# A two-level Winograd projection: two more of q, k and v's seven products split into quarters

## The chip, the cores and the metric

One core of a Trainium2 chip runs the whole kernel. The metric is the time on the device, in microseconds (us); lower is better. Five engines work in parallel, each in the order of its own instruction list: TensorE (PE, matmuls into PSUM, with its weight loads shown as PEld), VectorE (DVE), ScalarE (ACT), GpSimd (POOL) and SyncE (SP, which issues the DMAs). They wait for each other through semaphores.

## The reference

64 batches of 256 nodes with 512 features pass two layers. Layer 0 multiplies by an adjacency matrix and a weight; layer 1 is masked attention with 8 heads of 64 features. Each layer has a layer norm and a ReLU in front and a residual around it.

```python
h = jnp.maximum(_layernorm(x, axis=-1), 0.0)
x = x + (jnp.einsum('bnd,do->bno', jnp.einsum('nm,bmd->bnd', adj, h), weight) + bias)
h = jnp.maximum(_layernorm(x, axis=-1), 0.0)
q = (h @ Wq + bq).reshape(b, n, H, HD)      # k and v likewise
scores = jnp.einsum('bqhd,bkhd->bhqk', q, k) / jnp.sqrt(jnp.float32(HD))
scores = scores + (1.0 - adj)[None, None, :, :] * -1000000000.0
attn = jax.nn.softmax(scores, axis=-1)
x = x + (jnp.einsum('bhqk,bkhd->bqhd', attn, v).reshape(b, n, d) @ Wo + bo)
```

All is float32.

## The kernel before

Batches go in groups of two (`GB`), so there are 32 groups (`NG`). Layer 0 runs over all groups first and leaves two results in DRAM per group: the residual and the transposed hidden activations. Layer 1 then runs over the groups. In iteration g it does, in this order: `attend(g, 0)`, loads by DMA, `score(g, 1)`, `queries_keys(g + 1)` (first q, then k), `attend(g, 1)`, `score(g + 1, 0)`, `values(g + 1)`, and `post(g)`, the output product. On TensorE a group is thus six stretches: q, k, attention, v, output product, attention.

Every 512 by 512 product of a weight with two batches is done by the Winograd form of Strassen's method: the weight and the activations are cut in halves (blocks a11 to a22 and b11 to b22), sums s1 to s4 and t1 to t4 of blocks are made once, and seven products of half size take the place of eight. A half-size product is four matmuls of 128 rows by 256 columns (`product`). From group 2 (`FIRST2`) on, `project2` does three of the seven (a12 b21, a22 t4 and s4 b22) by the same method once more: each becomes seven matmuls of 128 columns, on quarter blocks (`W2` for the weight, `Blocks` for the activations). `block_sums` makes the sums of the weight's quarters, once for each weight, in the tiles of `spare`; POOL makes those of the activations for each group (`block_hidden`, `block_outputs`).

Matmuls write to PSUM, which has eight banks; `bank` takes the one that has been free longest, `give` returns it. A result leaves a bank through ACT (`first`, which adds the bias of q and k) or through DVE (`add`, onto what is there already). `bank(..., seed=...)` lets ACT copy values into a bank, onto which matmuls then accumulate.

The order is written by hand. A `yield` in a projection ends a step; `run` calls `tick` after each, and `after(delay, fn)` puts work of other engines into the instruction list that many ticks later. What is placed like this around the projections:

- `score`: 16 matmuls into eight banks, DVE scales and masks each (`scalar_tensor_tensor`, L980), POOL subtracts `top` in four pieces (L986), ACT takes the exponentials (`exponent`, at the ticks of `exps`, 3, 4, 5 and 8), POOL adds pairs of keys (`key_sum`, L998).
- `attend`: the sums of the exponentials (pden) and the weighted values (po, two banks), TensorE. ACT copies pden to `den`, DVE inverts it in four pieces (`invert`, L1027), two of them at once and the others in `divide`, one tick later, which also makes the two quotients oT (L1045) and gives back po's banks. ACT's `note` reads the inverses for a check of range.
- The loads of h1T (hidden) and x1 (residual) rotate through four buffers of `xpool`.

Of the kernel before, what the change touches and what calls it, by code (L numbers as in the profile page):

```python
# [198 lines left out]
def kernel(  # L199
# [35 lines left out]
    dram = main.enter_context(tc.tile_pool(name="between", bufs=1, space=bass.MemoryType.DRAM))  # L235
    xpool = main.enter_context(tc.tile_pool(name="x", bufs=4))
    act = main.enter_context(tc.tile_pool(name="act", bufs=1))
# [10 lines left out]
    def bank(shape, name, seed=None):  # L248

        i = next(i for i in free_banks if seed is None or whole[i])  # L250
        free_banks.remove(i)
        t = psum.tile(shape, F32, tag=f"bank{i}", name=name)
        bank_of[id(t)] = (i, t)
        if seed is not None:
            nc.scalar.copy(t, seed[:, None, :].to_broadcast(shape))
        return t
# [34 lines left out]
    def load(g):  # L291
        X[g] = xpool.tile([P, T, D], F32, tag="x", name=f"x_{g}")
        for k in range(GB):
            for i in range(NI):
                nc.sync.dma_start(blocks_of(X[g], i, k), by_block(x[g * GB + k], i))
# [74 lines left out]

    L1 = {}

    def load_layer1(n):
        w, bias = {"q": (wq, bq), "k": (wk, bk), "v": (wv, bv), "o": (wo, bo)}[n]
        if n in "qk":
            L1[n] = load_weight(nc, const, w, f"w{n}_sb"), load_column(nc, const, bias, f"b{n}_c")
        elif n == "v":
            L1[n] = load_weight(nc, const, w, "wv_sb"), None
        else:


            bv_c = const.tile([P, DC], F32, name="bv_c")
            wo_sb = const.tile([P, DC, D], F32, name="wo_sb")
            wo_v = w.rearrange("(q h f r) o -> h r q f o", q=HQ, h=4, f=2)
            bv_v = bv.rearrange("(q h f r) -> h r q f", q=HQ, h=4, f=2)
            for h in range(4):
                for q in range(HQ):
                    nc.sync.dma_start(wo_sb[32 * h:32 * h + 32, 2 * q:2 * q + 2, :], wo_v[h, :, q])
                    nc.sync.dma_start(bv_c[32 * h:32 * h + 32, 2 * q:2 * q + 2], bv_v[h, :, q])
            L1[n] = wo_sb, load_row(nc.sync, const, bias, "bo_r"), bv_c  # L390
# [119 lines left out]

    def block_sums(n):

        todo = []
        for a in ONCE:
            w = W[n][a]
            def part(i, j):
                return w[:, j, i * P:(i + 1) * P]
            s1, s2, s4 = (spare.pop(0) for _ in range(3))
            W2[n, a] = dict(a11=part(0, 0), a12=part(0, 1), a22=part(1, 1), s1=s1, s2=s2, s3=part(1, 0), s4=s4)
            for o, p, q, op in ((s1, part(1, 0), part(1, 1), ALU.add), (s2, s1, part(0, 0), ALU.subtract),  # L520
                                (part(1, 0), part(0, 0), part(1, 0), ALU.subtract), (s4, part(0, 1), s2, ALU.subtract)):
                todo.append((nc.gpsimd.tensor_tensor, o, p, q, op))
        return todo

# [15 lines left out]

    def project2(n, halves, blocks, by_token, name, place, first, done=None, seeds=(), add_up=False):

        s = W[n]

        def part(t, i, k):

            m, h = (k, i) if by_token else (i, k)
            t = t if m is None else t[:, m:m + 1, :]  # L550
            return t.rearrange("p m (h j) -> p (m h) j", j=P) if h is None else t[:, :, h * P:(h + 1) * P]

        class Inner:
# [103 lines left out]
        for p, c in zip(inner, ((0, 0), (1, 0), (0, 1))):  # L657
            p.u3()
            p.add(p.sum, None, 1)
            give(p.shared, False)  # L660
            complete(*c)
        yield

# [189 lines left out]

    H1T, HH, HO = {}, {}, {}

    def load_hidden(g):
        H1T[g] = xpool.tile([P, GB, DC, N], F32, tag="x", name=f"h1T_{g}")
        for k in range(GB):
            nc.sync.dma_start(H1T[g][:, k].rearrange("p d n -> p (d n)").rearrange("p (i n) -> p i n", n=N // NI),
                              HT[g][:, :, :, k, :].rearrange("p d i n -> p (d i) n"))  # L860

    def load_residual(g):
        X[g] = xpool.tile([P, T, D], F32, tag="x", name=f"x1_{g}")
        nc.sync.dma_start(X[g], X1[g].rearrange("k (t p) d -> p (k t) d", p=P))
# [7 lines left out]
    H2, O2 = {}, {}  # L872

    def block_hidden(g, step):

        t = act.tile([P, GB, 4, P], F32, tag="t2", name=f"t2_{g}")
        t4 = act.tile([P, 4, P], F32, tag="t24", name=f"t24_{g}")
        x = H1T[g][:, :, 2:4, :].rearrange("p k c (n j) -> p k c n j", j=P)
        H2[g] = block_sums_of(x, t, HH[g], t4, nc.gpsimd, step)

# [10 lines left out]
    def block_sums_of(x, t, halves, t4, eng, step):  # L891
# [4 lines left out]
        return {"b21": Blocks(x[:, 0], t[:, 0]), "b22": Blocks(x[:, 1], t[:, 1]), "t4": last}  # L896

    def queries_keys(g):

        for n, store in (("q", Q), ("k", K)):  # L900
            store[g] = {}
            bias = L1[n][1]

            def first(o, ps, i, m=None):
                for c in range(2) if m is None else (m,):
                    to, src = (o[:, c, :], ps[:, c, :]) if m is None else (o, ps)
                    nc.scalar.activation(to, src, AF.Identity, bias=bias[:, 2 * i + c:2 * i + c + 1])

# [4 lines left out]

            if g < FIRST2:
                yield from project(W[n], HH[g], False, f"{n}_{g}", place, first)
            else:
                yield from project2(n, HH[g], H2[g], False, f"{n}_{g}", place, first)

    def values(g):
        v = act.tile([P, HQ, GB, NT, HF], F32, tag="yT0", name=f"v_{g}")  # L920
        V[g] = {(i, k): v[:, i, k] for i in range(HQ) for k in range(GB)}

        def first(o, ps, i, m=None):
            nc.scalar.copy(o, ps)

        def place(i, k):
            return V[g][i, k]

        if g < FIRST2:
            yield from project(W["v"], HH.pop(g), True, f"v_{g}", place, first)  # L930
        else:
            yield from project2("v", HH.pop(g), H2.pop(g), True, f"v_{g}", place, first)

# [30 lines left out]
    def score(g, qd, sum_delay, exps=(3, 4, 5, 8)):  # L964
# [3 lines left out]
        for c in range(2):  # L968
            for b in range(GB):
# [13 lines left out]
                if (g == NG - 1 or (g, qd) == (0, 0)) and c + b == 2:  # L983
                    after(2, lambda a: nc.vector.tensor_tensor(a, a, top_b, op=ALU.subtract), a)  # L984
                else:
# [14 lines left out]
    def attend(g, qd):  # L1000
# [25 lines left out]
        def invert(c):  # L1026
            nc.vector.reciprocal(rden[:, c * P:(c + 1) * P], den[:, c * P:(c + 1) * P])  # L1027

        early = 2 if g >= FIRST2 and (g, qd) != (NG - 1, 1) else 4
        for c in range(early):  # L1030
            invert(c)
        if qd == 0:

            last = g == NG - 1
            OT[g] = (xpool if last else act).tile([P, DC, GN], F32, tag="x" if last else "r", name=f"oT_{g}")
            HO[g] = Halves(f"o_{g}", [OT[g][:, :, k * N:(k + 1) * N] for k in range(GB)], 0 if last else 1)
# [4 lines left out]
        def divide():  # L1041
            for c in range(early, 4):
                invert(c)
            for f in range(2):
                nc.vector.tensor_tensor(OT[g][:, 2 * qd + f, :], po[f], rden, op=ALU.mult)  # L1045
                give(po[f])
            after(2 if (g, qd) == (NG - 1, 1) else 3, note)
            wait = 0
# [4 lines left out]
            elif g == NG - 2:  # L1053
                wait = 8
                after(7, HO[g].sums, nc.gpsimd, ("t3",))
                after(8, HO[g].sums, nc.vector, ("t2",))
                after(8, HO[g].sums, nc.gpsimd, ("t4",))
            else:
                HO[g].sums(nc.vector, ("t3", "t2"))
                HO[g].sums(nc.gpsimd, ("t4",))  # L1060
            if qd and g >= FIRST2:
                block_outputs(g, nc.gpsimd, wait + 1 if g >= NG - 2 else 2)

        after(1, divide)

# [70 lines left out]
    for g in range(NG):  # L1136
        attend(g, 0)
        load_residual(g)
        if g + 2 < NG:
            load_hidden(g + 2)  # L1140
        score(g, 1, *((5,) if g < NG - 1 else (3, (3, 4, 5, 6))))
        tick()
        if g == 0:
            for n, tag in ((4 * DC, "w0_sb"), (4, "w0_s1"), (4, "w0_s2"), (4, "w0_s4"), (4, "adjT"), (4, "b0_r")):
                t = const.tile([P, n, P], F32, tag=tag, name=f"spare_{tag}")
                spare.extend(t[:, i, :] for i in range(n))
        for n, at in (("q", 7),) if g == 0 else (("k", 1), ("v", 5)) if g == 1 else (("o", 2),) if g == 2 else ():
            for i, work in enumerate(block_sums(n)):
                after(at + i // 3, *work)
        if g + 1 < NG:  # L1150
            run(queries_keys(g + 1))
        else:
            last = post(g - 1, seed_outputs(g - 1))
            run(last, 6)
        attend(g, 1)
        if g + 1 < NG:
            score(g + 1, 0, 5)
            tick()
# [57 lines left out]
```

## Time and profile before

| | |
|---|---|
| median of three runs | 2659.16 us (2658.59 to 2660.33) |
| profiled execution | 2660.45 us, its span 2658.7 us |
| granted TensorE clock, mean | 0.999 |
| DMA | 211.04 MB, mean 79 GB/s |
| one group of layer 1 (g=14, 1488.47 to 1551.47) | 63.00 us: busy PE 63.00, DVE 43.71, ACT 21.29, POOL 47.03 |
| POOL's longest idle time in it, ahead of `score(14, 0)` | 15.11 us, until DVE's masked scores |

The span goes from the first to the last instruction of one profiled execution. Times inside it are counted from its start. A matmul's line in a timeline gives the start and the time until its result is there; matmuls overlap, so that the distance of two starts is the pace. Each float32 matmul shows as two passes, so x2 is one matmul of the code. A note such as "[0.58 <-POOL as L998]" gives the idle time ahead of an instruction and what ended it.

### The profile page before, as it was taken

What the parts mean: (1) busy time and instruction counts of PE and PEld (TensorE: products, weight loads), DVE (VectorE), ACT (ScalarE), POOL (GpSimd) and SP (SyncE); (2) the same over time, 40 slices, a digit from 0 to 9 for tenths busy, and PEclk for the clock granted to TensorE, in tenths of its full rate; (3) what the DMA queues carried; (4) which work ended last, traced back from release to release, by engine and by line L of the source; (5) the groups of instructions that cost most, each with busy time, mean ns of one, the idle gap of its engine ahead of it and who ended that gap; (6) DMA issues with size and microseconds to landing.
All of it is one profiled execution on the core that took longest, in us unless ns stands there. A gap on an engine that the chain in (4) does not pass through costs nothing. (4 is left out here: it accounts for less than half of the span.)

```text
span 2658.7 us, 51781 instructions
## 1 busy us (share of the span) xinstructions
PE 2624.0 (99%) x20076; PEld 2282.2 (86%) x20076; DVE 1869.5 (70%) x3864; ACT 970.5 (37%) x1875; POOL 1981.1 (75%) x1838
## 2 busy tenths in 40 slices
PE   7999999999999999999999999999999999999997
PEld 6999899998888888888888888888888888888886
DVE  5878888885467676667677676667677676666677
ACT  3445454443333333333333333333333333333332
POOL 5888888775788777777777777777777777777775
PEclk9999999999999999999999999999999999999999
DMA  5777666665122111111111111111222111111110
GB/s 132 199 193 187 172 166 175 175 158 127 34 60 51 49 49 48 49 49 49 49 48 49 49 49 49 49 48 51 62 66 62 50 49 48 49 49 49 49 48 34
DMA packets 281066, 211.04 MB, mean 79 GB/s; under 512 B 145904, under 2 KB 212976, under 8 KB 280816
## 3 DMA queue, kind: packets, MB, share of 16 engines
q1 hardware_dynamic: 280352, 207.15, 29.9%
q8 instruction: 161, 2.64, 0.4%
q14 instruction: 89, 0.73, 0.1%
q10 hardware_dynamic: 464, 0.52, 0.1%
HBM read 106.96 MB, written 100.66 MB: 78 GB/s over the span
## 5 line engine op out<-in xcount | busy, mean ns | idle before, releaser
L986 POOL TENSOR_TENSOR a<-a,top 128x1024 f32<-128x1024 f32 x253 | 591.2, 2369 | 478.0 <-DVE a L980 478.0
L980 DVE SCALAR_TENSOR_TENSOR a<-sc,maskT 128x512 f32<-128x512 f32 x512 | 311.8, 680 | 122.8 <-PE sc L974 122.8
L998 POOL TENSOR_TENSOR as<-a 128x512 f32<-128x512 f32 x256 | 318.5, 1276 | 3.0 <-ACT a L991 3.0
L991 ACT ACTIVATE a<-a 128x1024 f32<-128x1024 f32 x256 | 270.9, 1058 | 4.3 <-DVE a L984 2.3
L1027 DVE RECIPROCAL rest<-rest 128x128 f32<-128x128 f32 x256 | 224.3, 919 | 36.1 <-ACT rest L1023 36.1
L974 PE MATMUL sc<-q,k 64*128 64x256 f32 x2048 | 239.0, 383 | 0.0
L1014 PE MATMUL pav<-a,v 128*32 128x256 f32 x4096 | 233.6, 379 | 0.0
L974 PEld LDWEIGHTS sc<-q,k 64*128 64x128 f32 x2048 | 194.7, 187 | 44.9 <-issue 26.3
L1014 PEld LDWEIGHTS pav<-a,v 128*32 128x32 f32 x4096 | 133.4, 110 | 87.9
L1023 ACT ACTIVATE rest<-pden 128x512 f32<-128x512 f32 x64 | 38.2, 597 | 417.7 <-PE pden L1007 417.7
L665 DVE TENSOR_TENSOR k<-k,k 128x128 f32<-128x128 f32 (+1 forms) x300 | 96.0, 352 | 126.3 <-PE k L564 123.9
L42 DVE BATCH_NORM_STATS2 st<-x 128x6 f32<-128x512 f32 x256 | 173.1, 676 | 9.4 <-DMA x<-in_x_dram 7.2
L693 ACT ACTIVATE h<-x,nb,rs 128x512 f32<-128x512 f32 x128 | 93.9, 803 | 69.3 <-POOL nb L54 69.2
L820 ACT ACTIVATE h<-x,nb,rs 128x512 f32<-128x512 f32 x128 | 97.2, 808 | 52.2 <-POOL nb L54 49.0
L665 DVE TENSOR_TENSOR x<-o,x 128x128 f32<-128x128 f32 (+1 forms) x360 | 110.9, 349 | 3.4 <-PE o_24b L564 0.3
L665 DVE TENSOR_TENSOR q<-q,q 128x128 f32<-128x128 f32 (+1 forms) x300 | 96.0, 352 | 14.0 <-PE q L564 11.7
L665 DVE TENSOR_TENSOR v<-v,v 128x128 f32<-128x128 f32 (+1 forms) x300 | 95.3, 351 | 14.4 <-PE v L564 11.3
L754 POOL TENSOR_TENSOR hs<-h 128x512 f32<-128x512 f32 x31 | 39.4, 1270 | 73.8 <-ACT h L693 63.7
L446 POOL TENSOR_TENSOR t_o<-oT,t_o 128x512 f32<-128x512 f32 x62 | 79.2, 1277 | 12.3 <-DVE t_o L446 10.0
L446 POOL TENSOR_TENSOR t_y<-yT 128x512 f32<-128x512 f32 (+1 forms) x65 | 81.8, 1258 | 5.9 <-ACT yT L804 5.9
L446 POOL TENSOR_TENSOR t_h<-h1T,t_h 128x512 f32<-128x512 f32 x64 | 82.0, 1282 | 5.0
L52 POOL TENSOR_TENSOR rs<-rs,mhalf 128x2 f32<-128x2 f32 (+1 forms) x97 | 79.5, 820 | 8.1
(4808 smaller groups left out, 6981.8 us busy)
## 6 DMA issues: line engine op xcount, KB each, us to landing
x<-in_x_dram SPq DMA_DIRECT2D x256, 128.0 KB, 3.1
residual<-x SPq DMA_DIRECT2D x256, 128.0 KB, 2.5
hidden<-r SPq DMA_DIRECT2D x128, 256.0 KB, 4.4
h1T<-hidden SPq DMA_DIRECT2D x64, 512.0 KB, 9.7
x<-residual SPq DMA_DIRECT2D x32, 1024.0 KB, 7.7
out_dram<-x SPq DMA_DIRECT2D x62, 512.0 KB, 4.3
w_sb<-in_L_gnn_weight_dram SPq DMA_DIRECT2D x1, 1024.0 KB, 9.8
wq_sb<-in_L_gnn_Wq_dram SPq DMA_DIRECT2D x1, 1024.0 KB, 8.2
```

Of the source, the lines that this page charges most:

```text
L42: nc.vector.bn_stats(st, src)
L446: eng.tensor_tensor(self.t[n][:, c, :], self.operand(p, c), self.operand(q, c), op=ALU.subtract)
L665: nc.vector.tensor_tensor(o, ps, u, op=ALU.add)
L693: nc.scalar.activation(H0[g][:, t, :], xt[:, t, :], AF.Relu, bias=nb[:, t % n:t % n + 1], scale=rs[:, t % n:t % n + 1])
L820: nc.scalar.activation(h1[:, k * NT + t, :], xt[:, k * NT + t, :], AF.Relu, bias=nb[:, t:t + 1], scale=rs[:, t:t + 1])
L974: nc.tensor.matmul(ps[j][:, kt * N:(kt + 1) * N], k[j * HD:(j + 1) * HD, c, kt * P:(kt + 1) * P], q[j * HD:(j + 1) * HD, c, :], start=(kt ...
L980: nc.vector.scalar_tensor_tensor(a[:, j * NT:(j + 1) * NT, :].rearrange("p k n -> p (k n)"), ps[j], SCALE, maskT_f, op0=ALU.mult, op1=ALU.add)
L986: nc.gpsimd.tensor_tensor(a, a, top_b, op=ALU.subtract)
L991: nc.scalar.activation(a, a, AF.Exp)
L998: nc.gpsimd.tensor_tensor(AS[c, b], a4[:, :, 0, :], a4[:, :, 1, :], op=ALU.add)
L1014: nc.tensor.matmul(po[f][h * 32:(h + 1) * 32, b * N:(b + 1) * N], v[:, k, h * HD + f * 32:h * HD + f * 32 + 32], A[h // 2, b][:, (h % 2) * ...
L1027: nc.vector.reciprocal(rden[:, c * P:(c + 1) * P], den[:, c * P:(c + 1) * P])
```

## The change

`project2` stays for the output product. For q, k and v of groups 2 to 31 a new `project3` does five of the seven half-size products on quarters: the three of before, and a11 b11 and s3 t3 (called A1 and A7). That leaves two half-size products, s2 t2 and s1 t1. The order of steps is new: A1, A7 and A3 (s4 b22) have their first quarter in one shared bank `sa`, their other parts in o1, o7 and o3; A2 and A4 share `s24` and o2, pc. The sum of A1 is put together in the output tile c00 and then copied back by ACT as the seed of bank pa, on which s2 t2 and s1 t1 accumulate; c11 likewise seeds pc. Since A1 and A7 are now taken separately, q's and k's second bias is a difference (`DIFF`).

```diff
+    def project3(n, halves, blocks, by_token, name, place, first):
+        s, part = W[n], part_of(by_token)
+
+        def mm(o, p, a, b, start=False):
+            lhs, rhs = W2[n, p][a], blocks[BUILT[p]].operand(b)
+            if by_token:
+                lhs, rhs = rhs, lhs
+            nc.tensor.matmul(o[:, 0, :], lhs, rhs, start=start, stop=True, skip_group_check=True)
+
+        def own(o, p, start=True):
+            mm(part(o, 0, 0), p, "a12", "b21", start)
+            mm(part(o, 0, 1), p, "s4", "b22")
+            mm(part(o, 1, 0), p, "a22", "t4")
+
+        def more(o, src, i, k):
+            o = part(o, i, k)
+            add(o, src if src.shape[1] == o.shape[1] else src.to_broadcast([P, o.shape[1], P]), o)
+
+        def take(o, src, i, k, h):
+            first(part(o, i, k), src, h, i)
+
+        def own_added(o, t):
+            more(o, part(t, None, 0), None, 0)
+            more(o, part(t, 1, 1), 1, 0)
+
+        def own_taken(o, t, h):
+            first(part(o, None, 1), part(t, None, 1), h, None)
+            give(t)
+
+        c00, c01, c10, c11 = (place(i, k) for i in range(2) for k in range(2))
+        sa = bank([P, 4, P], f"{name}s")
+        a1, a7, a3 = (sa[:, i:i + 1, :] for i in range(3))
+        mm(a1, "a11", "a11", "b11", True)
+        mm(a7, "s3", "a11", "b11")
+        o1 = bank([P, 2, N], f"{name}o1")
+        own(o1, "a11")
+        o7 = bank([P, 2, N], f"{name}o7")
+        own(o7, "s3")
+        take(c00, a1, 0, 0, 0)
+        take(c11, a7, 0, 0, 1)
+        yield
+        mm(a3, "s4", "a11", "b11")
+        mm(a1, "a11", "s2", "t2")
+        mm(a7, "s3", "s2", "t2")
+        mm(part(o1, 1, 1), "a11", "s3", "t3")
+        mm(part(o7, 1, 1), "s3", "s3", "t3")
+        o3 = bank([P, 2, N], f"{name}o3")
+        own(o3, "s4")
+        take(c00, a1, 1, 0, 0)
+        take(c11, a7, 1, 0, 1)
+        take(c01, a3, 0, 0, None)
+        for o, t, h in ((c00, o1, 0), (c11, o7, 1)):
+            own_added(o, t)
+            own_taken(o, t, h)
+        yield
+        mm(a1, "a11", "s1", "t1")
+        mm(a7, "s3", "s1", "t1")
+        mm(a3, "s4", "s2", "t2")
+        mm(part(o3, 1, 1), "s4", "s3", "t3")
+        more(c00, a1, None, 1)
+        take(c01, a3, 1, 0, None)
+        pa = bank([P, 2, N], f"{name}a", seed=c00)
+        more(c11, a7, None, 1)
+        yield
+        o2 = bank([P, 2, N], f"{name}o2")
+        own(o2, "a12")
+        s24 = bank([P, 4, P], f"{name}s24")
+        a2, a4, c4 = (s24[:, i:i + 1, :] for i in range(3))
+        mm(a4, "a22", "a11", "b11", True)
+        mm(a2, "a12", "a11", "b11")
+        mm(a3, "s4", "s1", "t1")
+        take(c10, a4, 0, 0, None)
+        pc = bank([P, 2, N], f"{name}c", seed=c11)
+        more(c00, a2, 0, 0)
+        yield
+        product(pa, s, "s2", halves, "t2", by_token, start=False, stop=False)
+        first(part(c10, 1, 0), part(pa, 1, 0), None, 1)
+        first(part(c10, None, 1), part(pa, None, 1), None, None)
+        more(c10, part(pa, 0, 0), 0, 0)
+        own_added(c01, o3)
+        yield
+        own(pc, "a22", False)
+        mm(a2, "a12", "s2", "t2")
+        mm(part(o2, 1, 1), "a12", "s3", "t3")
+        mm(a4, "a22", "s2", "t2")
+        mm(c4, "a22", "s3", "t3")
...
+        own_taken(c01, o3, None)
+        more(c01, a3, None, 1)
+        give(sa, False)
+        yield
+        product(pa, s, "s1", halves, "t1", by_token, start=False)
...
```

The last two steps end with eleven more additions by DVE. Around the projection other work moves: the exponentials to later ticks, the quotient from one tick after `attend` to five (its two later inverses at ticks 1 and 4; A2's first addition stands between the last inverse and the quotient), the sums t11 and t33 for the new products on POOL, k's weight sums to DVE, and the order of the last group. h1T and x1 rotate through three buffers; the fourth keeps weight quarters.

```diff
-        score(g, 1, *((5,) if g < NG - 1 else (3, (3, 4, 5, 6))))
+        score(g, 1, *((7, (5, 6, 6, 7)) if second(g + 1) else (5,) if g < NG - 1 else (3, (3, 4, 5, 6))))
         tick()
+        if g + 2 < NG:
+            block_first(g + 2, 12)
...
+        delay = 5 if second(g + 1) else 4 if (g, qd) == (NG - 1, 0) else 1
...
-        after(1, divide)
+        if (g, qd) == (NG - 1, 1):
+            divide()
+        else:
+            if delay == 5:
+                after(1, invert, 2)
+                after(4, invert, 3)
+            after(delay, divide)
...
     def block_hidden(g, step):
 
+        H2[g]["t3"] = Blocks(HH[g].t["t3"].rearrange("p c (n j) -> p c n j", j=P),
+                             tmp.tile([P, 4, P], F32, tag="u", name=f"t33_{g}"))
+        after(step - 2, H2[g]["t3"].sums, nc.gpsimd)
...
-                wait = 8
-                after(7, HO[g].sums, nc.gpsimd, ("t3",))
-                after(8, HO[g].sums, nc.vector, ("t2",))
-                after(8, HO[g].sums, nc.gpsimd, ("t4",))
+                wait = 8 - delay
+                after(wait, HO[g].sums, nc.gpsimd, ("t3",))
+                after(wait, HO[g].sums, nc.vector, ("t2",))
+                after(wait, HO[g].sums, nc.gpsimd, ("t4",))
...
-            run(last, 6)
+            run(last, 5)
```

## The prediction

> **What bounds the kernel now.** I read the page's busy times first, then who waited for whom on TensorE, then the stretches of one group of two batches (g=14) by engine, then the timelines of its stages and of the last 60 us. The page:
>
> ```profile
> PE 2624.0 (99%) x20076; PEld 2282.2 (86%) x20076; DVE 1869.5 (70%) x3864; ACT 970.5 (37%) x1875; POOL 1981.1 (75%) x1838
> ```
>
> A busy share of 99% does not prove that TensorE is the limit, but the waits do: between 900 and 2600 us the list of TensorE's waits is empty. The stretches of one group are q, k, attention, v, output product, attention. Columns: time, then busy us (instructions) of PE, PEld, DVE, ACT, POOL.
>
> ```profile
> 1488.47:1500.17 11.70, 11.70 (x76) 10.87 (x75) 9.38 (x20) 7.25 (x16) 11.70 (x7) 1.00 0.60 119
> 1500.17:1511.86 11.69, 11.69 (x76) 10.75 (x74) 5.59 (x16) 4.61 (x11) 3.70 (x4) 1.00 0.00 0
> 1519.97:1531.67 11.70, 11.70 (x76) 10.88 (x75) 9.46 (x20) 7.29 (x15) 11.62 (x7) 1.00 0.00 1
> ```
>
> TensorE fills each; DVE is 80% busy in q and v, 48% in k. A group takes 63.0 us, so a shorter projection shortens the run by its own gain, as long as nobody makes TensorE wait. Its pace, from k's timeline (start, length; x8 is four matmuls in two passes each, x2 is one):
>
> ```profile
> 1500.17 1.89 PE L453 MATMUL k_14a<-h1T,wk_sb 128*128 128x256 f32 x8
> 1501.90 1.89 PE L453 MATMUL k_14c<-t_h,wk_sb 128*128 128x256 f32 x8
> ...
> 1505.36 0.38 PE L564 MATMUL k<-h1T,wk_sb 128*128 128x128 f32 x2
> 1505.58 0.39 PE L564 MATMUL k<-t_h,wk_sb 128*128 128x128 f32 x2
> ```
>
> Starts are 1.73 us apart for a product of four 256-column matmuls (0.4325 each) and 0.2225 us for one of 128 columns; a result is there 0.17 us after the next start. The four lines that decide how far the gain gets, around q's start at 1488.47 (DVE, DVE, POOL, ACT):
>
> ```profile
> 1486.06 4.87 DVE L980 SCALAR_TENSOR_TENSOR a<-sc,maskT 128x512 f32<-128x512 f32 x8 [2.01 <-PE sc L974]
> 1490.85 1.75 DVE L1027 RECIPROCAL rest<-rest 128x128 f32<-128x128 f32 x2
> 1488.40 9.32 POOL L986 TENSOR_TENSOR a<-a,top 128x1024 f32<-128x1024 f32 x4
> 1499.97 1.05 ACT L991 ACTIVATE a<-a 128x1024 f32<-128x1024 f32 x1
> ```
>
> DVE is busy with the scores until 2.4 us into q; POOL's four subtractions end 9.2 us into q, and the last exponential that needs them starts at 11.5. At the end of the run TensorE does wait:
>
> ```profile
> 2614.67 1.89 PE L453 MATMUL o_30c<-wo_sb,t_o 128*128 128x256 f32 x8
> 2620.59 3.56 PE L453 MATMUL o_30a<-wo_s,t_o 128*128 128x256 f32 x8 [4.03 <-DVE x L665]
> ...
> 2632.13 0.41 PE L1007 MATMUL pden<-as,ones 128*32 128x256 f32 x2 [0.58 <-POOL as L998]
> ```
>
> **The Trainium skill.** TensorE: Matmul & The Clock Gate, section "Wait — 56ns, not 53.3ns?", gives a fixed cost of about 2.5 ns per matmul beside its columns: halving columns nearly halves time. The trace agrees: 111 ns per 128-column pass, 216 per 256. The same page, "Why this matters for your kernels", warns of TensorE gaps above about 3 us, after which the clock is halved: agrees, the eight passes after the 4.03 us gap took 3.56 us where 1.89 is usual. PSUM — Partial Sum Buffer, "PSUM bank collisions raise a hardware error", says that two engines must not touch one bank at once, reads included, and that dependencies are added for it; so ACT and DVE take turns on a bank. In the trace DVE's add from k_14a waits for ACT's copy out of the same bank at 1511.70.
>
> **The gain.** project2 has four 256-column products (16 matmuls) and 21 small ones: 16 x 0.4325 + 21 x 0.2225 = 11.59 us, and 0.10 at the change of shape before q and v or behind k: the measured 11.70 and 11.69. project3 has 8 and 35: 3.46 + 7.79 = 11.25. Gain 0.345 per projection, 1.035 per group, over 30 groups (2 to 31) 31.1 us.
>
> **What it costs other engines**, per projection. DVE: 21 additions for 15. Spacings in the trace are 0.20, 0.33 and 0.60 us for 128, 256 and 512 columns (0.47 for 384): before 6, 6 and 2 and one of 384, 4.9 us; now 8, 9 and 4, 7.0. ACT: q and k 16 operations for 10, v 14 for 7, among them two seeds of 0.52: 1.2 to 1.4 us more. POOL: six more quarter sums per group, two sets of 1.76 us (the row of such a set runs 1486.64 to 1488.40). Per group DVE goes from 43.7 to about 50, POOL 47.0 to 50.5, ACT 21.3 to 25, of some 62.5. No engine becomes the bound by its sum. The order does matter.
>
> **The hand-over in q.** Times from q's first matmul; an engine starts 0.04 us after the one it waits for (the trace has 0.03 to 0.11). Step 1 (8 small matmuls) ends at 1.88, step 2 at 3.66, step 3 at 4.55. DVE is free of the scores and of one reciprocal at 3.25. It adds o1's two quarters, the second dependent on the first (0.42, 0.28): 3.98. ACT takes o1's other half in two biased pieces: 4.64. DVE adds A1's half: 5.09. ACT may then read the same bank for A3: 5.39. DVE adds A7's half, again from that bank: 5.85. Only then may TensorE write A3's third product there, at 5.90. It arrives at 5.66 (step 3, then 5 matmuls). Stall 0.24. The seed of pa (ACT, 5.29 to 5.87) is in time; later waits have 0.4 us or more.
>
> **In k** DVE is late from q's last additions (free at 14.3); the chain starts with ACT at the same time, and the same counting gives 0.14. ACT first has to be free: POOL's subtractions now start 1.76 later for the t3 set, plus what v saves, at 1.83, the fourth ends at 11.15; last exponential to 12.1, the note to 12.7, two pieces of A1 and A7 to 13.36. TensorE wants that bank at 13.37: 0.03. **In v** ACT's pieces are single copies: 0.11. Left per group 1.035 - 0.24 - 0.17 - 0.11 = 0.52, over 30 groups 15.5 us.
>
> Bounds: with no stall 1.035; with hops of 0.08 instead of 0.04, at some seven hops each (0.33, 0.26 and 0.21 of stall), and POOL 0.5 later, the stalls reach 1.3 and the group loses 0.3. I take 0.52, as most waits in the trace end within 0.04 us.
>
> **Moved work.** The quotient (two of 0.65, behind a reciprocal) goes from 4.2 us into v to 6.8 to 8.1. It holds two PSUM banks four steps longer: project3 needs sa, o1, o7, o3 before o1 is given back, and six are free. POOL's sums of oT start, as before, when its subtractions end at 8.3: nothing, by 0.2 us. If that cover went, POOL has 1.4 us until pden wants its key sums. h1T and the residual have three buffers for four: h1T(g+2) now follows post(g-1)'s output DMA (4.3 us) on SP's queue, and is wanted some 40 us later by POOL: nothing. t11 lies in POOL's 15 us gap before the scores: nothing. The quarter sums of weights (72 small operations for 48; k's on DVE) fall in groups 0 to 2, where POOL had about 10 us free per group: I take 1 us, between 0 and 5.
>
> **The tail.** The third product of o_30 waited for DVE's add, queued behind a sum of oT (1.87), two reciprocals and two quotients (3.04). These now come before or after it, so the 4.03 us and the 1.7 us of slow clock behind it go. Next late is pden, which waits for POOL's key sums: before, POOL ran without a gap from 2611.71 to 2632.08 (20.4 us). In the new order one sum and the rest set (5 us) lie ahead of the scores, in its idle time, so pden ends some 5 us sooner; but TensorE gets there at about 2621 and stands for about 6 us, with the slow clock again. I take 4 us, between 0 and 6.
>
> **Sum.** -15.5 - 4 + 1 = -18.5 us on the profiled execution of 2660.45 (span 2658.7 and 1.75 around it): 2642. The median of the runs shown is 2659.16, 1.3 lower: 2640.7. Forecast 2641.
>
> **Rivals.** (1) TensorE never stalls: 2659.2 - 31.1 - 4 + 1 = 2625. For it: most hops are 0.03 to 0.05 and DVE might start the chain earlier where it is free; against it: the bank's turns are fixed by the order and DVE's scores end when they do. (2) The hand-over eats all: at 0.345 of stall per projection, only the tail is left: 2656. For it: seven hops in a row, each under-counted by 0.03, are enough for two of the three. Against it: the measured waits. (3) The slower one: POOL is later than I count, so the last exponential, first in ACT's queue ahead of k's first two pieces, holds TensorE at k's second step. One us of lateness is one us per group, since ACT works in order and the cover is used up to 0.03. From 0.65 us per group it decides; at 1.0 us the run is 2641 + 30 = 2671. For it: POOL ran without a gap from v's scores to q's, and already began q's subtractions late; against it: its durations are steady and v's end relieves it. That the change does not do what it says can be left out: the matmul counts are those of the code.
>
> **Chances.** Forecast 0.47, (1) 0.18, (2) 0.18, (3) 0.17. Under 0.2% (5.3 us, about what a measurement of this kernel can tell from no change) counts as same: from (2) half, slightly from the others, 0.13. Faster is most of the forecast, all of (1) and a third of (2): 0.70; slower 0.17. The range leaves out half of each end: 2624 to 2668; the forecast's own is 2630 to 2652.
>
> **What would show it.** q, k and v in about 11.6, 11.4 and 11.5 us; small TensorE waits for DVE at A3's last product in q, k and v; none, or one for ACT, at k's second step; none at o_30a's third product, one of some 6 us at pden in the tail. DVE near 80% busy. I am wrong if ACT waits for POOL grow before k, or if the stalls in q and v exceed 0.35.

## The result and the profile after

The changed kernel takes 2661.77 us (median of 12 runs, 2661.18 to 2664.87), the kernel before 2659.73 us (12 runs, 2658.17 to 2662.27). The ratio is 1.0009, with an interval of 1.0001 to 1.0016: no gain, and if anything a loss of 2 us. The prediction said 2641.

TensorE's line of the page is as before, to 0.3 us of busy time, although it now has some 31 us less to multiply by the prediction's count; DVE, ACT and POOL have grown by what was expected.

```profile
PE 2623.7 (99%) x21156; PEld 2297.9 (86%) x21156; DVE 2074.5 (78%) x4423; ACT 1084.6 (41%) x2445; POOL 2082.8 (78%) x2029
```

The stretches of the same group of two batches, in the columns of before (q, k, attention, v, output product, attention), show where the time is:

```profile
1491.45:1503.20 11.75, 11.65 (x89) 11.05 (x87) 10.35 (x25) 8.48 (x20) 11.59 (x8) 1.00 0.50 113
1503.20:1514.93 11.73, 11.65 (x89) 10.92 (x87) 8.06 (x22) 5.64 (x19) 6.88 (x8) 1.00 0.00 1
1514.93:1523.04 8.11, 8.11 (x114) 5.53 (x113) 6.69 (x13) 0.69 (x2) 1.05 (x1) 1.00 0.01 2
1523.04:1534.68 11.64, 11.64 (x89) 11.03 (x87) 10.36 (x25) 7.76 (x19) 11.56 (x7) 1.00 0.01 3
1534.68:1546.42 11.74, 11.74 (x77) 10.66 (x75) 9.02 (x23) 1.83 (x4) 11.43 (x13) 1.00 0.00 0
1546.42:1554.53 8.11, 8.11 (x114) 5.53 (x113) 5.80 (x12) 0.69 (x2) 7.72 (x10) 1.00 0.70 228
```

q, k and v take 11.75, 11.73 and 11.64 us, where before had 11.70, 11.69 and 11.70: together 35.12 for 35.09, although each has 0.345 us less to multiply. The output product, whose code is the same, takes 0.05 more than before, where it was

```profile
1531.67:1543.36 11.69, 11.69 (x76) 10.74 (x75) 7.86 (x22) 0.75 (x1) 11.38 (x13) 1.00 0.00 1
```

A group takes 63.08 us for 63.00.

TensorE's timeline at the end of q's fourth step shows the loss (start, time to the result; the last two lines are A3's third product and s2 t2):

```profile
1496.70 0.39 PE L689 MATMUL q_14s<-t_h,wq_sb 128*128 128x128 f32 x2
1496.93 0.39 PE L689 MATMUL q_14s<-h1T,wq_sb 128*128 128x128 f32 x2
1497.41 0.49 PE L689 MATMUL q_14s<-t,spare_w_sb 128*128 128x128 f32 x2
1497.73 0.60 PE L457 MATMUL q_14a<-t_h,wq_s 128*128 128x256 f32 x2
```

Starts of 128-column products lie 0.22 us apart. A3's third product comes 0.48 after the one ahead of it, so TensorE stood for 0.26. Then s2 t2 comes 0.32 after that, not 0.22: another 0.10. No note says "idle" on these lines, because idle time is counted from the modelled result (0.39 after the start) and only 0.09 is left of it. Read from starts, the same place in k loses 0.25 + 0.10 and in v 0.17 + 0.10:

```profile
1508.58 0.39 PE L689 MATMUL k_14s<-h1T,wk_sb 128*128 128x128 f32 x2
1509.05 0.49 PE L689 MATMUL k_14s<-t,spare_w_s 128*128 128x128 f32 x2
1509.37 0.60 PE L457 MATMUL k_14a<-t_h,wk_s 128*128 128x256 f32 x2
1528.50 0.39 PE L689 MATMUL v_14s<-wv_sb,h1T 128*128 128x128 f32 x2
1528.89 0.49 PE L689 MATMUL v_14s<-spare_x,t 128*128 128x128 f32 x2
1529.21 0.38 PE L457 MATMUL v_14a<-wv_s,t_h 128*128 128x256 f32 x1
```

The three together are 0.98 us per group, out of a counted gain of 1.035.

What TensorE waited for is in DVE's and ACT's timelines of the same time. L793 is `add`, L1059 and L1056 are pieces taken by `first3`, L255 is the seed of a bank.

```profile
1494.68 1.35 DVE L793 TENSOR_TENSOR q<-q_14o,q 128x256 f32<-128x256 f32 x4
1496.12 0.42 DVE L793 TENSOR_TENSOR q<-q_14s,q 128x256 f32<-128x256 f32 x1
1496.93 0.42 DVE L793 TENSOR_TENSOR q<-q_14s,q 128x256 f32<-128x256 f32 x1 [0.39 <-ACT q L1056]
```

```profile
1495.46 0.62 ACT L1059 ACTIVATE q<-q_14o,bq_c 128x128 f32<-128x128 f32 x2 [0.48 <-DVE q L793]
1496.12 0.62 ACT L1059 ACTIVATE q<-q_14o,bq_d 128x128 f32<-128x128 f32 x2
1496.63 0.27 ACT L1056 COPY q<-q_14s 128x128 f32<-128x128 f32 x1
1496.78 0.61 ACT L255 COPY q_14a<-q 128x512 f32<-128x512 f32 x1
```

DVE, ACT, DVE, ACT, DVE take turns: o1's additions, o1's pieces (1495.46 to 1496.08), A1's half (to 1496.54), A3's piece (1496.63 to 1496.90), A7's half (1496.93 to 1497.35), and TensorE at 1497.41. The seed of pa, which s2 t2 needs, ends at 1497.39, at the same time.

At the end of the run the order of waits has changed as expected, the sum hardly:

```profile
PE pden L1160 <- POOL as L1151: 5.6, 4, 4.4
PE o L578 <- DVE x L793: 1.1, 3, 0.7
PE v_31s L689 <- DVE v L793: 0.4, 1, 0.4
```

Before, pden's waits were

```profile
PE pden L1007 <- POOL as L998: 2.9, 3, 1.3
```

The 4.03 us at the third product of o_30 are gone; a single wait of 4.4 at pden stands in their place, and the waits of v_31 and o for DVE are new. From v_31's first product to the last matmul of the run it is 59.48 us, before 60.54.

The account: from q_2 to q_31 the changed kernel takes 1830.91 us, before 1827.96 (+2.95, 0.10 per group); from q_31 to v_31 +0.09; the tail -1.06; ahead of q_2 the distance from the first pden is 73.15 for 73.16. Together +2.0, and the medians differ by 2.0. What lies ahead of the first pden is left out; it differs by 1.7 us between these two profiled executions, and over all runs here it varies by 4 us.

### The profile page after: what moved, and what is told of

Read it like the earlier page. It is cut to its first block, busy times and chain, and to the rows that moved or that the text cites. A ratio compares the mean times of both kernels' runs of the same rounds, so it can differ in the third digit from the quotient of the medians.

```text
span 2662.6 us, 54815 instructions
## 1 busy us (share of the span) xinstructions
PE 2623.7 (99%) x21156; PEld 2297.9 (86%) x21156; DVE 2074.5 (78%) x4423; ACT 1084.6 (41%) x2445; POOL 2082.8 (78%) x2029
## 5 line engine op out<-in xcount | busy, mean ns | idle before, releaser
L1180 DVE RECIPROCAL rest<-rest 128x128 f32<-128x128 f32 x260 | 235.6, 930 | 19.8 <-ACT rest L1176 19.8
L793 DVE TENSOR_TENSOR x<-o,x 128x128 f32<-128x128 f32 (+1 forms) x360 | 111.1, 350 | 3.1
L954 DVE STREAM_TRANSPOSE r<-h 128x512 f32<-128x512 f32 x128 | 82.8, 684 | 2.3 <-ACT h L948 1.7
L450 POOL TENSOR_TENSOR t_y<-yT,t_y 128x512 f32<-128x512 f32 (+1 forms) x65 | 81.8, 1259 | 2.4
L450 POOL TENSOR_TENSOR t_o<-oT 128x512 f32<-128x512 f32 x63 | 81.9, 1300 | 0.4 <-DVE oT L1199 0.4
```

Of the source, the lines that this page charges most:

```text
L450: eng.tensor_tensor(self.t[n][:, c, :], self.operand(p, c), self.operand(q, c), op=ALU.subtract)
L793: nc.vector.tensor_tensor(o, ps, u, op=ALU.add)
```

## The experiments

Theory A: TensorE loses the gain at one place, the turns on bank `sa` in step four of `project3`, and pays 0.10 more whenever it has stood. Rival B: POOL and ACT as a whole hold it, so that whatever is won at that place comes back as another wait. Rival C: the smaller products are not faster. All ratios below are to the kernel before, run on the same chip. The experiments ran on three chips, so what they gain over the changed kernel is read from the stretches of their traces.

**e1, one product ahead.**

```diff
+        mm(part(o2, 1, 1), "a12", "s3", "t3")
         mm(a3, "s4", "s1", "t1")
         take(c10, a4, 0, 0, None)
...
         mm(a2, "a12", "s2", "t2")
-        mm(part(o2, 1, 1), "a12", "s3", "t3")
```

> The small product o2(1,1) of A2 is issued ahead of A3's third product instead of behind s2 t2; nothing else changes. Theory A (TensorE loses its gain at the turns on bank sa: 0.26, 0.25 and 0.17 us of wait in q, k, v, and 0.10 more whenever it has stood): it comes there 0.22 later, so 0.04 and 0.03 of wait (with the 0.10) stay in q and k and none in v; 0.22 + 0.22 + 0.27 = 0.71 per group, 21 over 30 groups: 2640 us. Rival B (TensorE is held by the queue of POOL and ACT as a whole, not by this bank): the last exponential, which follows POOL, ends 0.46 ahead of TensorE's need in k; v and q gain 0.49 before it, so k waits there instead; at least 2646. Rival C (the 0.345 is no gain at all, the pace is another): 2662.

Measured 2648.76 us, ratio 0.9957 (0.9943 to 0.9970). Medians over the groups, from the starts: q 11.53, k 11.52, v 11.42, that is 0.22, 0.21 and 0.22 less than in the changed kernel, against 0.22, 0.22 and 0.27 expected. In q the product starts 0.26 after the one ahead, 0.04 late, and the next one 0.33 after it: the 0.10 is paid in full after a stop of 0.04. The output product, which no theory had touched, is 0.14 longer (11.88); that is most of the 0.20 per group that is missing. C falls. The times of e1, e2 and e4 alone lie in B's ranges; only the stretches tell A from B. B's wait in k's second step does not show here.

**e2, two products ahead.** As e1, with `mm(c4, "a22", "s3", "t3")` moved in the same way.

> Two small products, o2(1,1) and c4, are issued ahead of A3's third product. Theory A: the wait there goes in all three (0.36, 0.35 and 0.27 with the 0.10), but the step behind s2 t2 is 0.45 shorter, so that s1 t1 comes to bank pa 0.05 before DVE has read it: 0.05 + 0.10 in each; left 0.53 per group: 2646 us. Were bank pa free in time, 2632. Rival B: the wait moves to k's second step, 2650 or more. Rival C: 2662.

Measured 2654.80 us, ratio 0.9982 (0.9975 to 0.9989), 9 us over A's 2646. The wait at A3 is gone, and s1 t1 waits at bank pa in q, k and v, 0.06 + 0.10, where A had 0.05 + 0.10; q 11.56, k 11.55, v 11.53. The output product is at 11.94, 0.20 worse, which A had not counted. A move that empties one step starves the next.

**e3, the third product behind s2 t2.** It is issued after `product(pa, s, "s2", ...)`, the seed of pa is left where it is.

> A3's third product is issued behind s2 t2 instead of before it, so that it cannot wait for the turns on bank sa. Theory A says that the seed of pa, which ACT copies in the same chain, ends at the same time as DVE's addition of A7 (in q 1497.38 against 1497.35): s2 t2 now waits for the seed, 0.27, 0.25 and 0.19, with the 0.10: no change, 2660 to 2664 us, and the trace names ACT where it named DVE. If the bank's turn alone held TensorE, 2633.

Measured 2664.66 us, ratio 1.0020 (1.0012 to 1.0028), just above the range expected. TensorE and ACT in q:

```profile
1494.86 0.39 PE L689 MATMUL q_14s<-h1T,wq_sb 128*128 128x128 f32 x2
1495.38 1.99 PE L457 MATMUL q_14a<-t_h,wq_s 128*128 128x256 f32 x8
```

```profile
1494.72 0.61 ACT L255 COPY q_14a<-q 128x512 f32<-128x512 f32 x1
```

s2 t2 starts 0.05 after the seed's end, 0.30 late, and its eight passes take 0.10 more than the usual 1.89. Two guards stood side by side: with the bank's turn out of the way, the seed costs as much, and 0.03 more in each projection (11.78, 11.77 and 11.67).

**e4, third product behind s2 t2, seed first, two products ahead.**

```diff
-        take(c01, a3, 1, 0, None)
         pa = bank([P, 2, N], f"{name}a", seed=c00)
+        take(c01, a3, 1, 0, None)
...
-        mm(a3, "s4", "s1", "t1")
+        mm(part(o2, 1, 1), "a12", "s3", "t3")
+        mm(c4, "a22", "s3", "t3")
         take(c10, a4, 0, 0, None)
...
         product(pa, s, "s2", halves, "t2", by_token, start=False, stop=False)
+        mm(a3, "s4", "s1", "t1")
```

> A3's third product behind s2 t2, o2(1,1) and c4 ahead of it in its place, and ACT copies the seed of pa before it takes A3's second product. Theory A: the seed is ready 0.2 before TensorE needs it; no wait in q and v (0.36 and 0.27 gained), k is held by 0.17 at its second step by the last exponential (cover 0.46, used up by 0.63) and pays 0.10 more: about 0.71 per group, 2640 us; 2632 if that exponential is in time. Rival B: 2650 or more. Rival C: 2662.

Measured 2652.82 us, ratio 0.9971 (0.9960 to 0.9982), 13 us over A's 2640. q 11.39 and v 11.37: there the whole gain arrives. But k is at 11.91. TensorE there, and ACT:

```profile
1498.86 0.39 PE L689 MATMUL k_14o<-t,wk_sb 128*128 128x128 f32 x2
1499.49 0.49 PE L689 MATMUL k_14s<-h1T,wk_s 128*128 128x128 f32 x2 [0.24 <-ACT k L1059]
1499.81 0.39 PE L689 MATMUL k_14s<-t,spare_w_s 128*128 128x128 f32 x2
```

```profile
1497.26 1.06 ACT L1144 ACTIVATE a<-a 128x1024 f32<-128x1024 f32 x1 [0.51 <-POOL a L1139]
1498.22 0.61 ACT L1193 ACTIVATE rest<-rest 128x512 f32<-128x512 f32 x1
1498.83 0.35 ACT L1059 ACTIVATE k<-k_14s,bk_c 128x128 f32<-128x128 f32 x1
1499.08 0.35 ACT L1059 ACTIVATE k<-k_14s,bk_d 128x128 f32<-128x128 f32 x1
```

The last exponential waits for POOL (0.51), the note follows, and only then ACT takes k's first pieces; k's second step, due at 1499.08, starts at 1499.49: 0.41 + 0.10, where A had 0.17 + 0.10. This is B's mechanism, and it decides only once q and v are shorter. The output product has its 0.14 here too.

**e5, that exponential two ticks later.** `exps` ahead of q from `(5, 6, 6, 7)` to `(5, 6, 6, 9)`, on e4.

> e4_behind_seed with the last exponential ahead of k two ticks later, behind the pieces that ACT takes in k's first step. Theory: what stood in k of e4 (11.91 us for 11.38) was ACT's queue, the exponential that follows POOL's last subtraction standing ahead of k's first pieces; k falls to about 11.4, q, v and o stay at 11.39, 11.37 and 11.88: 0.5 per group, 2637 us. Rival: POOL as a whole is late, and the wait comes back at the sums of keys or at the scores: 2648 or more.

Measured 2637.73 us, ratio 0.9918 (0.9904 to 0.9931). k 11.38, the rest unchanged. It was the place of the exponential in ACT's queue, not POOL's load.

**e6, v's last two additions behind o's first.**

```diff
-        more(c00, a2, None, 1)
-        more(c10, a4, None, 1)
-        give(s24, False)
+        def last():
+            more(c00, a2, None, 1)
+            more(c10, a4, None, 1)
+            give(s24, False)
+
+        if by_token:
+            after(2, last)
+        else:
+            last()
```

> As e5, and v's last two additions come behind the output product's first one in DVE's order. Theory: the output product's 0.14 us more in e1 and e4 (11.88 for 11.74) is its third product, which waits until DVE, still with v's last additions, has read its bank; o falls to 11.70 to 11.75: 4 to 5 us less than e5, about 2632. Rival: DVE as a whole is behind, and a later product of o waits in its place: as e5.

Measured 2632.59 us, ratio 0.9899 (0.9884 to 0.9914). Its stretches, in the columns of above:

```profile
1476.92:1488.32 11.40, 11.40 (x89) 10.99 (x88) 10.14 (x25) 8.34 (x21) 11.24 (x8) 1.00 0.53 115
1488.32:1499.70 11.38, 11.38 (x89) 10.85 (x87) 7.97 (x23) 6.03 (x18) 7.90 (x9) 1.00 0.00 0
1499.70:1507.81 8.11, 8.11 (x114) 5.53 (x113) 6.82 (x13) 0.69 (x2) 1.05 (x1) 1.00 0.01 2
1507.81:1519.18 11.37, 11.37 (x89) 10.96 (x87) 10.13 (x25) 7.57 (x18) 10.98 (x7) 1.00 0.01 3
1519.18:1530.87 11.69, 11.69 (x77) 10.74 (x75) 9.16 (x24) 2.05 (x5) 11.38 (x12) 1.00 0.00 0
1530.87:1538.98 8.11, 8.11 (x114) 5.53 (x113) 5.79 (x12) 0.69 (x2) 7.72 (x10) 1.00 0.74 242
```

A group takes 62.06 us, 0.94 less than before, with DVE's, ACT's and POOL's busy time within 0.3 us of the changed kernel's (50.02, 25.37, 50.28). The output product is back at 11.69. With the same work on each engine, what was missing was order, not capacity.

**e7, the tail.** On e6, in the last group only: DVE's subtraction of top a tick earlier, POOL's sum t1 of oT behind the sums of keys.

```diff
-                    after(2 if g == 0 else 4 + 2 * (1 - qd), lambda a: nc.vector.tensor_tensor(a, a, top_b, op=ALU.subtract), a)
+                    after(2 if g == 0 else 3 + 3 * (1 - qd), lambda a: nc.vector.tensor_tensor(a, a, top_b, op=ALU.subtract), a)
...
-                HO[g].sums(nc.gpsimd, ("t1",))
+                after(2, HO[g].sums, nc.gpsimd, ("t1",)) if g == NG - 1 else HO[g].sums(nc.gpsimd, ("t1",))
```

> As e6, with two moves in the last group alone: DVE's subtraction of top one tick earlier, and POOL's sum t1 of the last oT behind the four sums of keys. Theory: the wait of 4.4 us at pden in the tail is the chain DVE, ACT, POOL; the sums end some 2.5 us sooner: about 2.5 us less than e6 (1 to 4), groups before unchanged. Rival: the scores and exponentials set the time: no change.

Measured 2630.67 us, ratio 0.9888 (0.9873 to 0.9903), the fastest of all. TensorE's longest waits at the end:

```profile
PE pden L1167 <- POOL as L1158: 3.1, 4, 1.6
PE o L578 <- DVE x L800: 1.6, 3, 1.3
PE v_31s L689 <- DVE v L800: 0.6, 1, 0.6
```

The longest wait at pden falls from 4.6 in e6 to 1.6; v_31 to the last matmul is 57.31 us for 59.95, 2.64 less. Part of that is the clock: behind e6's wait it was granted at 0.50 (2598 to 2602) and 0.76 (2602 to 2606), behind e7's at 1.00. In return the waits of o for DVE grow from 0.5 to 1.6. The four sums of keys now run without a break:

```profile
2596.79 4.95 POOL L1158 TENSOR_TENSOR as<-a 128x512 f32<-128x512 f32 x4
```

In the changed kernel one sum of keys was followed by a gap and by t1, and the other three ended 7.55 us after the first began. The medians show 1.9 of the 2.6, and the intervals of e6 and e7 overlap: the trace, not the time, carries this one.

**e8, the quotient back in its old place.**

```diff
-        delay = 5 if second(g + 1) else 4 if (g, qd) == (NG - 1, 0) else 1
+        delay = 4 if (g, qd) == (NG - 1, 0) else 1
```

> The changed kernel with one part undone: the quotient and both last reciprocals right behind the scores again, as in the kernel before. If the hand-over of q and v starts when DVE comes free, as the prediction counted it, it starts 0.87 + 1.29 = 2.2 us later in both: 4.3 per group, 130 us over 30 groups, about 2790 us. If DVE's place has little to do with the waits: within 10 us of 2662.

Measured 2812.84 us, ratio 1.0576 (1.0560 to 1.0592). The medians of q and v are 13.94 and 13.69, 2.19 and 2.05 more than in the changed kernel, where 2.2 each was expected; k stays at 11.73. So the hand-over starts when DVE comes free, and without the moved quotient the change would lose 150 us. Two stops at A3's third product:

```profile
1520.52 0.80 PE L689 MATMUL v_13s<-spare_x,t 128*128 128x128 f32 x2 [2.06 <-DVE v L793]
1521.11 3.28 PE L457 MATMUL v_13a<-wv_s,t_h 128*128 128x256 f32 x8
...
1555.96 0.49 PE L689 MATMUL q_14s<-t,spare_w_sb 128*128 128x128 f32 x2 [2.28 <-DVE q L793]
1556.28 1.89 PE L457 MATMUL q_14a<-t_h,wq_s 128*128 128x256 f32 x8
```

After the first, the eight passes take 3.28 us for the usual 1.89 (granted clock 0.58 from 1520.4 to 1524.5); after the second, longer one, they do not (1.00 from 1555.9 to 1558.2). Read from starts, the slow stretch costs 1.7 us. It follows 17 of the 58 stops from group 3 on: some 27 us, enough for the 23 over the expectation.

**e9, a bank of its own for A3, in k alone.**

```diff
-        a1, a7, a3 = (sa[:, i:i + 1, :] for i in range(3))
+        s3 = bank([P, 4, P], f"{name}s3") if n == "k" else sa
+        a1, a7, a3 = sa[:, 0:1, :], sa[:, 1:2, :], s3[:, 2:3, :]
```

> The changed kernel, but in k alone A3's first quarter has a bank of its own; A1 and A7 keep sa. Order of all instructions as before. Theory: the wait at A3's third product is the turns of ACT and DVE on one bank, not the data of A3, which ACT has read 0.5 us before; k's wait there goes (0.25), and as s2 t2 then comes when its seed ends (1509.03 in the trace of the changed kernel, TensorE there at 1509.03), at most 0.05 and the 0.10 of restart stay: k 11.73 to 11.4 or 11.5, q, v and o unchanged, 7 to 10 us less than the changed kernel: 2652 to 2655. Rival: A3's own data or DVE's speed is what TensorE waits for; k unchanged, 2662.

Measured 2657.28 us, ratio 0.9989 (0.9982 to 0.9995). k falls to 11.54 (0.19 less), q, v and o are unchanged.

```profile
1504.82 0.39 PE L689 MATMUL k_14s<-t,spare_w_s 128*128 128x128 f32 x2
1505.12 1.99 PE L457 MATMUL k_14a<-t_h,wk_s 128*128 128x256 f32 x8
```

The 0.25 at A3's third product (first line) is gone, so it was the shared bank, not A3's data; s2 t2, right behind, now waits 0.08 for its seed and pays the 0.10. I expected at most 0.05 there and 7 us or more in all; it is 0.19 per group, 5.7 by the trace, 5.3 by the two ratios.

## Why the prediction was wrong

**The bound** was right: TensorE sets the time in both kernels. **The gain** of 0.345 per projection was right within 0.03: without a stop q, k and v take 11.39, 11.38 and 11.37 in e6, which is 0.31 to 0.33 less than before: 0.94 per group, not 1.035.

**The hand-over** is the step that failed, and in its size only. It was put at the right matmul, with the right chain of engines. In q the stall of 0.24 was measured as 0.26. In k 0.14 (and 0.03 for a late ACT) was 0.25: DVE's first addition came at 1506.26, right behind ACT's piece of A1, and ACT took that piece at 1505.86, 0.04 after the result not of A1's second product but of A7's, which goes to the same bank. The 0.03 did not come: ACT had k's first pieces done 0.46 ahead of TensorE. In v 0.11 was 0.17, and no single hop stands out. The three sum to 0.68 for 0.49. The prediction's own bad case is not worked out right either: seven hops of 0.08 for 0.04 add 0.28 to each stall, but the stalls in its brackets (0.33, 0.26 and 0.21) are only 0.09 to 0.12 above the forecast's.

**The missing term** is the other half. The prediction charged a stop with its length. Each of these stops also costs 0.10 us at the next matmul, whether it is long or short (0.26, 0.25 and 0.17 here, 0.04 in e1's q, 2.28 in e8): 0.30 per group. It had been seen, but it was booked as the price of a change of shape only. With it, 0.68 + 0.30 = 0.98 are gone, more than the 0.94 won, where 0.52 were to be left. Another 0.05 goes at the output product's third product, whose eight passes take 1.94 for 1.89: DVE, with more of v's additions in front, has only just read its bank; e6 brings it back. So 0.94 - 0.98 - 0.05: a group loses 0.1 instead of gaining 0.5. That is the rival in which the hand-over eats all, and its reason, hops under-counted in two of three projections, is half of what happened.

**The moved work** came at nothing, as said: the quotient (e8 has the price of its old place, 4.2 us per group), POOL's sums, the three buffers. The weights' quarter sums cost nothing ahead of q_2, where 1 us was taken. DVE, ACT and POOL are at 50.27, 25.09 and 50.23 us per group; 50, 25 and 50.5 had been worked out.

**Rival 3**, POOL late and k's second step held by the last exponential, did not come true in the changed kernel, whose q and v are no shorter. It is real: e4 has it at 0.41 + 0.10, and e5 takes it away.

**The tail** brought 1.06 us, not 4. The wait of 4.03 went, and 4.4 at pden came, with a slower clock behind it (granted 0.76 from 2630 to 2634, 0.87 from 2634 to 2640), as foreseen. Not foreseen were v_31's wait of 0.37 behind DVE's subtraction of top, now later in its queue, and the three waits for DVE of 1.1 at o_30's last products, behind the quotient and the sums that had been put ahead of o_30's additions.

By the trace: predicted -15.5 - 4 + 1, measured +3.04 - 1.06 + 0.

Not tried: which of the hops in k and v are longer than counted, one by one (what is said of k above is read from one trace); whether the last 0.10 before pden and at the start of q and v can be avoided.

## What to carry to other kernels

When two engines hand one PSUM bank to and fro ahead of a matmul, count the last of the waits that guard the place, not the first: here the bank's turn and the seed ended within 0.04 us of each other, and removing one alone gave nothing (e3) or half (e9). Fill the wait with matmuls from a later step that depend on none of it, then read every stretch again, because the shortened stages use up cover elsewhere: in k the exponential, in the output product an addition. On a TensorE that is 99% busy, look for lost time in the distances of starts, since the list of waits does not show a stop of 0.26 us and the busy time shows only 0.10 of it.

## What the hardware showed that I had not expected

**A stop costs up to 0.10 us beyond its length.** After the stops read above, from 0.04 us (e1, q) to 2.28 us (e8), the first matmul takes 0.32 to the next start instead of 0.22, or eight passes 1.99 instead of 1.89. It can be less: in e1's v, A3's third product starts in time and takes 0.04 longer, and the output product's third product starts 0.12 late in e1 and takes 0.07 longer. The Trainium skill, TensorE: Matmul & The Clock Gate, "Step-by-step: what each phase is for", says that in a stream the drain of one matmul lies under the next, while an isolated one can't hide it. That fits, but no run here shows that it is the reason, and the figure given there, 219 cycles, stands in a formula for the slow clock and is no price for these stops.

**The clock can fall after 2.06 us of standing.** The same page, section "What's actually happening", says that an idle window of about 3.4 us brings the slow clock and that the window runs freely, so that it depends on where a gap falls in it. The second part agrees with e8: of 58 stops of 2.05 to 2.56 us only 17 were followed by slow matmuls, and the one of 2.28 shown above was not. The length doesn't: 2.06 of idle time (2.22 from starts) was enough. The measurement decides; the prediction's "about 3 us" was too generous a limit.
